# Four graph layers with pre-norm on one core: the normed inputs of layers 1 and 2 go through memory to be transposed

## The chip, the cores and the metric

The kernel runs on one core of one Trainium2 chip. The time is that of one execution on the device, in microseconds. The core has five engines that run side by side, each strictly in its own order: TensorE (PE, with its weight loads listed as PEld), VectorE (DVE), ScalarE (ACT), GpSimd (POOL) and SyncE (SP), which here does nothing but issue DMAs. They wait for each other by semaphores. [...]

## What is computed

There are 64 graphs of 256 nodes with 128 features, in fp32, and one adjacency matrix of 256 x 256 for all. Four layers follow each other; each adds its result to x, and each starts with the same norm:

```python
h = maximum(layernorm(x), 0); x = x + L0(h)   # and so on for L1, L2, L3
# L0: pre = s1[:, :, None] + s2[:, None, :] + b   (256 features, all pairs of nodes)
#     attn = softmax(sum_e a_e * leaky(pre_e) + adj);  sigmoid(attn @ h)
# L1: x_h = elu(h @ Wi + bi); e = sigmoid(a_tgt + a_src + be) * mask(adj)
#     recv = elu([e @ x_h, x_h * rowsum(e)] @ Wn + bn);  [recv, x_h] @ Wm + bm
# L2: A = exp(8 tanh(h q (h k)^T / sqrt(128) / 8)) * adj;  (A / rowsum(A)) @ h @ v
# L3: 5 steps of a gated unit: m = adj @ h; z, r = sigmoid(..); h = (1 - z) h + z tanh(..)
```

Layer 0 is by far the largest part: for every pair of nodes and each of 256 features a maximum has to be formed before the features are summed.

## The kernel before

**Groups and layers.** The 64 graphs are taken in 34 groups (`GROUPS`, line 15): 30 of two graphs, with two groups of one graph at each end. A group's x is a tile of 128 partitions x 4 blocks x 128 features; a block is half a graph's nodes. A `W` of 512 is the 4 blocks x 128 nodes of a group.

**Layer 0's pairs.** `Pairs` (from line 596) makes tiles `r` of 128 partitions x 256, each of them a maximum of `s2` and one column of `s1n`. Such a tile can be made by ACT (line 714), by POOL (719) or by DVE (696, eight or four at a time). A batch is eight tiles in one of `BUFS` = 12 buffers; PE multiplies a batch with `a_win` into `e_ps` (line 780). When `SPARE` = 5 batches are waiting for PE, the next two rows are merged: DVE adds the second feature's maximum onto the first (738), and PE has a batch less to do. `softmax0` then does the softmax, the product with h and the sum with x.

**Who sets the order.** The program is written out by a planner that runs when the kernel is built (the loop from line 1303). It has a clock for each of PE, DVE, ACT and POOL, charges each instruction a fixed cost, and always emits what can begin first. The work behind layer 0's pairs is written as generators ("chains") that yield the name of the engine they need next: `ahead` (norm and projections of the next group), `behind` (`softmax0`), `chain12` (layers 1 and 2), two `lanes` (layer 3 of even and odd groups) and two chains for the last two groups. A chain has a pace: its next step is due so many ns after the last one (2500 for `behind`, 2200 for `chain12`, 2100 for the lanes). A yield may name a condition and an earliest time. On the chip, each engine then keeps the emitted order, whatever is late.

**Transposes.** The products need h with features on the partitions, the norm leaves it with nodes there. The kernel has two ways:
- `transpose_blocks` (477): PE turns four blocks into PSUM (line 127), ACT copies them out (487). Layers 1 and 2 do so, each with its own norm `ln_relu` (442), as the first steps of `chain12`.
- `crossed` (89): SP issues a DMA that writes the tile to memory (`there`, line 93) and, when that has landed, a second DMA (95) that reads it back with the first two axes exchanged. For that the norm stores its output as features x blocks, `across=True`, so that the read moves 16 bytes (4 blocks) at a time. Layer 3 of groups 0 to 27 (`BY_MEMORY`, 26) does so, in `layer3_across` (1116): once behind its norm (`h3t`), and once at the end of each of four of the five steps (`hn`). After a crossing the planner lets the product that reads it begin no earlier than `TURN` = 28000 ns behind the producer. SP's DMAs are one queue in the order emitted: the loads of x, the crossings, the small `row` and `bound` transfers, and the writes of `out`.

**Tiles.** x lies in `xt` (line 140, five buffers). `softmax0` writes x1 over it; `layer1` makes `x1b` (x1 plus a bias, on POOL, line 900) and `x2`, `layer2` makes `x3`, layer 3 makes `y`, each a tile of its own. The adjacency is held twice: `adj_t` (columns half by half) for layers 1 and 2, and `adj_q` (node and half interleaved) for `layer3_across`. The helper `mm` (112) does each product as four products of 32 columns; in the trace an fp32 product shows as two records.

Of the kernel before, what the change touches and what calls it, by code (L numbers as in the profile page):

```python
# [24 lines left out]
TURN = 28000  # L25
BY_MEMORY = range(0, 28)
# [31 lines left out]
def kernel(ctx: ExitStack, tc: tile.TileContext, ins: dict, out: bass.AP):  # L58
# [127 lines left out]
    def numbers(shape, name, pattern, per_partition, t=None):  # L186
# [16 lines left out]
        for k, home in {  # L203
            "L2_gnn_q": ("hf_0", 2), "L2_gnn_k": ("hf_0", 2), "L3_gnn_w3_w": ("x1b",),
            "L3_gnn_w4_w": ("y1",), "L3_gnn_w5_w": ("x2",), "L3_gnn_u3_w": ("m_t",),
# [16 lines left out]
    adj_t = constant([P, 2, N], "adj_t")  # L222
    adj_q = constant([P, 2, P, 2], "adj_q")
    v2_rep = constant([P, P], "v2_rep")
# [6 lines left out]
    def constants0():  # L231
# [128 lines left out]
        t_ps = psum([P, 2, N], "adj_t_ps")  # L360
# [4 lines left out]
        dve(2 * N).tensor_copy(adj_t, t_ps)  # L365
# [13 lines left out]
    def constants1():  # L379

        for c in range(2):
            yield "dve"
            dve(N).tensor_copy(adj_q[:, :, :, c], adj_t[:, :, bass.ts(c, P)])
        yield "dve"

        dve(2 * N).tensor_scalar(mask_h, adj_t, 0.0, 0.5 * 0.005, ALU.is_equal, ALU.mult)
        yield "dve"
        dve(2 * N).scalar_tensor_tensor(mask_h, adj_t, 0.5, mask_h, ALU.mult, ALU.add)
# [24 lines left out]
        q_t, k_t = raw["L2_gnn_q"], raw["L2_gnn_k"]  # L413
        yield from transposed(q_t, q_t)
        yield from transposed(k_t, k_t)
        yield "pe"
        qk_ps = psum_a([P, P], "qk_ps")
        mm(qk_ps, lhsT=q_t, rhs=k_t, start=True, stop=True)
        yield "dve"
        dve(P).tensor_copy(qk, qk_ps)  # L420

        for k, t in ws.items():
            yield "dve"
            r = raw["L3_gnn_" + k]
            dve(P).tensor_tensor(r[:, 0:P], r[:, 0:P], r[:, P : 2 * P], ALU.add)
            yield from transposed(t, r[:, 0:P])
        yield from transposed(u3_t, raw["L3_gnn_u3_w"])
        yield from transposed(u5_th, raw["L3_gnn_u5_w"], 0.5)
        yield "dve"

        dve(P).tensor_tensor(w34_t, ws["w3_w"], ws["w4_w"], ALU.subtract)
        yield "dve"
        for t, a, b, scale in (
            (bz, "w3_b", "u3_b", 0.5), (br, "w4_b", "u3_b", 0.5), (bh, "w5_b", "u5_b", 1.0),
        ):
            dve(1).tensor_tensor(t, biases[a], biases[b], ALU.add)
            if scale != 1.0:
                dve(1).tensor_scalar(t, t, scale, None, ALU.mult)
# [346 lines left out]
    def softmax0(g, b, of, e_ps, snd):  # L785
# [43 lines left out]
        for ic in range(2):  # L829
# [5 lines left out]
        x1 = xt  # L835
        dve(N).scalar_tensor_tensor(
            x1[:, bass.ts(b, 2), :], o_ps, 0.5, xt[:, bass.ts(b, 2), :], ALU.mult, ALU.add
        )
        if b == GROUPS[g] - 1:
            chain12.add(first_rest(g, x1))  # L840
# [30 lines left out]
    def layer1(x1):  # L871
        G, NB, W = sizes(x1)
        h = yield from ln_relu(bp, x1, "h1", "h")
        h_t = yield from transpose_blocks(bp, h, "h_t", psum_a)
        yield "pe"
        xh_ps = psum_a([P, W], "xh_ps")
        mm(xh_ps, lhsT=wi, rhs=flat(h_t), start=True, stop=True)
        xh_t = yield from elu(xh_ps, bi, "xh_t", "xh_t")

        for b in range(NB):  # L880
# [17 lines left out]
        x1b = bp.tile([P, G, P], F32, tag="x1b", name="x1b")  # L898
        counts["x1"] += 1
        pool(1265).tensor_tensor(  # L900
            x1b, x1, bm_bc.unsqueeze(1).to_broadcast([P, G, P]), ALU.add
# [4 lines left out]
        for b in range(NB):  # L906
            yield "pe"
            th_ps = psum_a([P, 2, N], "th_ps")
            mm(th_ps[:, 0, :], lhsT=wt_rep, rhs=xh_t[:, bass.ts(b, N)], start=True, stop=True)
# [23 lines left out]
        for b in range(NB):  # L933
            for jc in range(2):
                mm(
                    rc_ps[:, bass.ts(b, N)], lhsT=y[:, b * 2 + jc, :], rhs=e_ts[b][:, jc, :],
                    start=(b == 0 and jc == 0), stop=False, skip_group_check=True,
                )
# [4 lines left out]
        for g in range(G):  # L943
            mm(
                o1_ps[:, g, :], lhsT=rc_t[:, bass.ts(g, P)], rhs=wm[:, 0, :], start=True, stop=False
            )
            mm(
                o1_ps[:, g, :], lhsT=xh_t[:, bass.ts(g, P)], rhs=wm[:, 1, :], start=False, stop=True
            )
        yield "dve"  # L950
        x2 = bp.tile([P, G, P], F32, tag="x2", name="x2")
        dve(W).tensor_tensor(x2, o1_ps, x1b, ALU.add)
        return x2

    def layer2(x2, when):
        G, NB, W = sizes(x2)
        h = yield from ln_relu(bp, x2, "h2", "h")
        h_t = yield from transpose_blocks(bp, h, "h_t", psum_a)
        yield "pe"
# [7 lines left out]
        for g in range(G):  # L967
            mm(hv_ps[:, g, :], lhsT=h_t[:, g, :], rhs=vw, start=True, stop=True)
# [5 lines left out]
        for b in range(NB):  # L974
            yield "pe"
            s_ps = psum_a([P, 2, N], "s2_ps")
            for mc in range(2):
                mm(
                    s_ps[:, mc, :], lhsT=h_t[:, b * 2 + mc, :], rhs=g_t[:, bass.ts(b, N)],
# [8 lines left out]
            dve(2 * N).tensor_tensor(pm, s_ps, adj_t, ALU.mult)  # L988
            pms.append(pm)
        for b in range(NB):  # L990
            yield "pe"
            o_ps = psum_a([P, 2, P + 1], "o2_ps")
            for c in range(2):
                for mc in range(2):
                    mm(
                        o_ps[:, c, :], lhsT=pms[b][:, mc, bass.ts(c, P)], rhs=hv[:, b * 2 + mc, :],
                        start=(mc == 0), stop=(mc == 1),
                    )
            yield "dve", when
            if b == 0 and when:  # L1000
                x3 = bp.tile([P, G, P], F32, tag="x3", name="x3", bufs=2)
            elif b == 0:
                x3 = rp.tile([P, G, P], F32, tag="r", name="x3")
            rv = sp.tile([P, 2], F32, tag="rv", name="rv")
            dve(2, more=120).reciprocal(rv, o_ps[:, :, P])
            for c in range(2):
                dve(P, 1).scalar_tensor_tensor(
                    x3[:, b * 2 + c, :], o_ps[:, c, 0:P], rv[:, c : c + 1],
                    x2[:, b * 2 + c, :], ALU.mult, ALU.add,
                )  # L1010
        return x3
# [26 lines left out]
    def layer3(x3, hn, h_t, home):  # L1038
        G, NB, W = sizes(x3)
        hf = flat(h_t)  # L1040
        for step in range(STEPS):
            yield "pe"
            m_ps = home.bank([P, W], "m_ps")
            for b in range(NB):
                for mc in range(2):
                    mm(
                        m_ps[:, bass.ts(b, N)], lhsT=hn[:, b * 2 + mc, :], rhs=adj_t[:, mc, :],
# [48 lines left out]
            if step < STEPS - 1:  # L1096
# [3 lines left out]
                for g in range(G):  # L1100
                    tr(tp[:, bass.ts(g, P)], hf[:, bass.ts(g, P)])
# [7 lines left out]
        for g in range(G):  # L1109
            tr(tp[:, bass.ts(g, P)], hf[:, bass.ts(g, P)])  # L1110
        yield "dve"
        y = home.tile(W, "hn", "y").rearrange("p (g n) -> p g n", g=G)
        dve(W).tensor_tensor(y, tp.rearrange("p (g n) -> p g n", g=G), x3, ALU.add)  # L1113
        return y

    def layer3_across(x3, lane):
# [64 lines left out]
        y = bp.tile([P, G, P], F32, tag="hn" + tag, name="y")  # L1181
        dve(W).tensor_tensor(y, tp, x3, ALU.add)
        inside.remove(lane)
        return y

    def first_rest(g, x1):
        x2 = yield from layer1(x1)

        x3 = yield from layer2(x2, None if g == len(GROUPS) - 1 else lambda: done3(g - 2))
        if g in BY_MEMORY:  # L1190
            lanes[g % 2].add(last_rest(g, x3))
            return
        tag = "_%d" % (g % 2)
        hn = yield from ln_relu(bp, x3, "h3", "hn" + tag, lambda: done3(g - 2))
        h_t = yield from transpose_blocks(bp, hn, "h3t", psum_a, tag="hf" + tag, bufs=2)
        lane = {len(GROUPS) - 1: chain5, len(GROUPS) - 2: chain4}.get(g, lanes[g % 2])
        lane.add(last_rest(g, x3, hn, h_t, Home(g)))
# [4 lines left out]
    def last_rest(g, x3, hn=None, h_t=None, home=None):  # L1202
        if home is None:
            y = yield from layer3_across(x3, g % 2)
        else:
# [5 lines left out]
            y = yield from layer3(x3, hn, h_t, home)  # L1211
            if not home.banks:
                inside.remove(g % 2)
        nc.sync.dma_start(out=of_group(out, g), in_=y)
        written.add(g)

    counts = {"w_p": 0, "left": 0, "x1": 0}
# [50 lines left out]
    lanes = [Chain(2100), Chain(2100)]  # L1268
# [34 lines left out]
    while True:  # L1303
        while to_load and counts["x1"] >= to_load[0] - 4:
# [111 lines left out]
```

## Time and profile before

| | us |
|---|---|
| median of 3 runs | 4993.88 (4990.81 to 4998.51) |
| the profiled execution, its own time | 4991.51 |
| its span (first to last instruction) | 4989.7 |
| PE busy | 4946.9 (99%) |
| DVE busy | 4865.1 (98%) |
| ACT busy | 4884.7 (98%) |
| POOL busy | 4771.1 (96%) |
| granted TensorE clock | 0.999 |

A line of the profile's groups has the source line, the engine, the operation, output<-inputs (buffer numbers left out), the shape and the count; behind the first bar the time in which the group was busy (us) and the mean duration of one (ns); behind the second the idle time of the engine just before them and what ended it. ACT and DVE overlap the end of one instruction with the beginning of the next, so the distance from start to start is shorter than the duration. In the timeline of SP the second column is how long the issue took; a DMA's data move after that.

The largest groups are the tiles of layer 0: 9944 on POOL (4520.5 us busy), 10232 on ACT (4541.5 us), 1351 instructions with 8 or 4 tiles each (2398.1 us) and 4168 merges (1729.2 us) on DVE, and 40816 records of their products on PE (3290.6 us). The DMA queue carries 140 crossings of 256 or 128 KB, each read in 16-byte or 8-byte packets: 2.29 of its 2.37 million packets.

### The profile page before, as it was taken

The numbers are of one execution on the slowest core, as the hardware profiler recorded it, in microseconds if no ns is written. First come the engines' busy times: TensorE is split into PE (matmuls) and PEld (weight loads), VectorE is DVE, ScalarE is ACT, GpSimd is POOL, SyncE is SP. The second block draws the span as 40 slices with busy tenths as digits, with TensorE's granted clock in tenths as the row PEclk, the third lists the DMA queues.
The fourth block names the chain that finished last, engine by engine and source line by source line (L and its number), as shares of the span: only waits on it lengthen the run. The fifth ranks groups of instructions, "written<-read, shape, count | busy, mean of one in ns | idle before, by whom it ended". The sixth has DMA issues, their size and how long they took to land. (4 is left out here: it accounts for less than half of the span.)

```text
span 4989.7 us, 176852 instructions
## 1 busy us (share of the span) xinstructions
PE 4946.9 (99%) x69759; PEld 2337.1 (47%) x69759; DVE 4865.1 (98%) x8327; ACT 4884.7 (98%) x12828; POOL 4771.1 (96%) x10569
## 2 busy tenths in 40 slices
PE   9999999999999999999999999999999999999997
PEld 4455444444544444444444444444454444444443
DVE  9999999999999999999999999999999999999994
ACT  8999999999999999999999999999999999999994
POOL 8999999999999999999999999999999999999882
PEclk9999999999999999999999999999999999999999
DMA  0144553654454555464444444353544434321000
GB/s 22 4 14 16 21 25 19 28 24 20 23 24 19 23 23 27 20 23 23 23 23 23 23 19 27 20 28 19 23 23 23 23 23 24 19 15 9 4 7 6
DMA packets 2372273, 100.40 MB, mean 20 GB/s; under 512 B 2318576, under 2 KB 2354800, under 8 KB 2371440
## 3 DMA queue, kind: packets, MB, share of 16 engines
q1 hardware_dynamic: 2370896, 88.83, 39.1%
q8 instruction: 547, 8.96, 0.9%
q14 instruction: 286, 2.34, 0.2%
q10 hardware_dynamic: 544, 0.26, 0.0%
HBM read 45.23 MB, written 43.84 MB: 18 GB/s over the span
## 5 line engine op out<-in xcount | busy, mean ns | idle before, releaser
L719 POOL TENSOR_SCALAR r<-s,s1n 128x256 f32<-128x256 f32 x9944 | 4520.5, 479 | 79.5 <-PE e_ps L780 36.1
L714 ACT ACTIVATE r<-s_act,s 128x256 f32<-128x256 f32 x9720 | 4226.5, 952 | 10.3 <-PE e_ps L780 10.0
L780 PE MATMUL e_ps<-r,a_win 128*32 128x256 f32 (+1 forms) x40816 | 3290.6, 465 | 5.5 <-DVE r L696 4.7
L696 DVE TENSOR_TENSOR r<-s_ps,s1n 128x2048 f32<-128x2048 f32 (+1 forms) x1351 | 2398.1, 1821 | 2.8 <-PE e_ps L780 2.6
L780 PEld LDWEIGHTS e_ps<-r,a_win 128*32 128x32 f32 x40816 | 1339.9, 110 | 1590.3 <-issue 846.0
L738 DVE SCALAR_TENSOR_TENSOR r<-s_ps,s1n,r 128x256 f32<-128x256 f32 x4168 | 1729.2, 485 | 2.9 <-POOL r L719 2.7
L714 ACT ACTIVATE r<-s,s 128x256 f32<-128x256 f32 x512 | 315.0, 1145 | 0.0
L120 PE MATMUL m_ps<-adj_q,hn 128*32 128x256 f32 x3456 | 209.2, 380 | 0.0
L120 PE MATMUL gate_ps<-m_t,t_w_w 128*32 128x512 f32 (+1 forms) x1360 | 170.6, 571 | 4.0 <-ACT m_t L1054 2.9
L120 PEld LDWEIGHTS m_ps<-adj_q,hn 128*32 128x32 f32 x3456 | 135.2, 135 | 79.2 <-issue 30.2
L471 ACT ACTIVATE h<-x,bsh,brs 128x128 f32<-128x128 f32 x256 | 159.0, 865 | 13.0 <-POOL bsh L464 9.0
L120 PE MATMUL hv_ps<-rh,u_th 128*32 128x512 f32 (+1 forms) x1360 | 169.6, 567 | 1.5 <-DVE rh L1067 1.5
L120 PE MATMUL gate_ps<-m_t,w_t 128*32 128x512 f32 (+1 forms) x1360 | 169.9, 568 | 0.7 <-ACT m_ps L1064 0.6
L120 PE MATMUL hv_ps<-m_t,t_w_w 128*32 128x512 f32 (+1 forms) x1360 | 170.1, 569 | 0.0
L471 ACT ACTIVATE h<-xt,bsh,brs 128x128 f32<-128x128 f32 x256 | 158.5, 916 | 3.8 <-POOL bsh L464 2.5
L1143 ACT COPY m_t<-m_ps 128x512 f32<-128x512 f32 (+1 forms) x140 | 159.9, 1142 | 0.0
L1159 ACT ACTIVATE gate_ps<-gate_ps,bz 128x512 f32<-128x512 f32 (+1 forms) x140 | 159.6, 1140 | 0.0
L1161 ACT ACTIVATE hv_ps<-hv_ps,bh 128x512 f32<-128x512 f32 (+1 forms) x140 | 153.4, 1096 | 0.0
L1147 ACT ACTIVATE m_ps<-gate_ps,br 128x512 f32<-128x512 f32 (+1 forms) x140 | 152.7, 1091 | 0.0
L120 PE MATMUL gate_ps<-hf,u_t 128*32 128x512 f32 (+1 forms) x1088 | 138.0, 575 | 0.0
L120 PE MATMUL s_ps<-h0t,w_p 128*32 128x256 f32 (+1 forms) x1568 | 134.7, 444 | 0.8 <-ACT h0t L487 0.5
L462 POOL TENSOR_TENSOR brs<-bve,neg_half 128x4 f32<-128x4 f32 (+1 forms) x136 | 133.7, 983 | 0.0
(231 smaller groups left out, 4527.8 us busy)
## 6 DMA issues: line engine op xcount, KB each, us to landing
there<-hf SPq DMA_DIRECT2D x104, 256.0 KB
hn<-there SPq DMA_DIRECT2D x104, 256.0 KB
xt<-in_x_dram SPq DMA_DIRECT2D x30, 256.0 KB
out_dram<-y SPq DMA_DIRECT2D x30, 256.0 KB
there<-h SPq DMA_DIRECT2D x26, 256.0 KB
h3t<-there SPq DMA_DIRECT2D x26, 256.0 KB
row<-rows SPq DMA_DIRECT2D x128, 0.5 KB
there<-hf SPq DMA_DIRECT2D x8, 128.0 KB
```

What stands on the lines that cost most here:

```text
L120: nc.tensor.matmul(out[bass.ts(c, 32)], lhsT=lhsT[:, bass.ts(c, 32)], rhs=rhs, **flags)
L462: pool(1085).tensor_tensor(rstd, ve, neg_half[:, 0:G], ALU.pow)
L471: act(P, 2, 1).activation(h[:, :, g] if across else h[:, g, :], xt[:, g, :], AF.Relu, bias=shift[:, g : g + 1], scale=rstd[:, g : g + 1],)
L696: nc.vector.tensor_tensor(r[:, 2 * g2 : 2 * g2 + n, :, :], s2[:, ec : ec + 1, :].unsqueeze(1).to_broadcast([P, n, 2, N]), s1n.to_broadcast ...
L714: nc.scalar.activation(r[:, g, ic, :], s2[:, ec, :], AF.Relu, bias=s1[:, ec, i : i + 1])
L719: nc.gpsimd.tensor_scalar(r[:, g, ic, :], s2[:, ec, :], FLT_MAX, s1n[:, ec, i : i + 1], ALU.min, ALU.max,)
L738: nc.vector.scalar_tensor_tensor(r[:, g, ic, :], self.own("dve")[:, 1, :], self.of["s1n"][:, 1, i : i + 1], r[:, g, ic, :], ALU.max, ALU.add,)
L780: nc.tensor.matmul(to, lhsT=a_win[:, sign, 31 - t : 63 - t], rhs=of, start=False, stop=self.over, skip_group_check=True,)
L1143: act(W).copy(m_t, m_ps)
L1147: act(W, 1).activation(m_ps, g_ps, AF.Tanh, bias=br, scale=0.5)
L1159: act(W, 1).activation(g_ps, g_ps, AF.Tanh, bias=bz, scale=0.5)
L1161: act(W, 1).activation(hv_ps, hv_ps, AF.Tanh, bias=bh)
```

## The change

Layers 1 and 2 of groups 0 to 31 get their transposed input by `crossed`; only the last two groups still use PE (`by_pe`). Layer 1's norm is now run at the end of `softmax0`'s chain (`first_norm`), which issues the crossing and then hands the rest to `chain12` with the earliest time of the first product. `TURN` goes from 28000 to 16000, for all crossings, layer 3's included. Layer 3 crosses in groups 0 to 28 instead of 0 to 27; the lanes' pace is 2300 instead of 2100.

As a crossing of 16-byte runs leaves node and block interleaved, all tiles of layers 1 and 2 are in that order now (`pairs`): weights such as `xh[:, :, g]` are read with a step, some products write PSUM with a step, and the masks come from `adj_q`; `adj_t` is gone. x1 plus bias, x2, x3 and y are written over x in `xt`, which has eight buffers instead of five; the load of a group's x waits until the group eight before it has been written out.

```diff
-TURN = 28000
-BY_MEMORY = range(0, 28)
+TURN = 16000
+BY_MEMORY = range(0, 32)
+BY_MEMORY_3 = range(0, 29)
...
-        xt = ap.tile([P, 2 * GROUPS[g], P], F32, tag="xt", name="xt", bufs=5)
+        xt = ap.tile([P, 2 * GROUPS[g], P], F32, tag="xt", name="xt", bufs=8)
...
         if b == GROUPS[g] - 1:
-            chain12.add(first_rest(g, x1))
+            yield from first_norm(g, xt)
...
-    def layer1(x1):
+    def layer1(x1, h, h_t, at):
         G, NB, W = sizes(x1)
-        h = yield from ln_relu(bp, x1, "h1", "h")
-        h_t = yield from transpose_blocks(bp, h, "h_t", psum_a)
-        yield "pe"
+        if h_t is None:
+            h_t = yield from by_pe(h, "h_t1")
+        yield "pe", None, at
         xh_ps = psum_a([P, W], "xh_ps")
         mm(xh_ps, lhsT=wi, rhs=flat(h_t), start=True, stop=True)
...
-                    y_ps[:, c, :], lhsT=xh_t[:, bass.ts(2 * b + c, P)], rhs=wn1,
+                    y_ps[:, c, :], lhsT=xh[:, :, 2 * b + c], rhs=wn1,
...
-                    rsum_ps[:, bass.ts(b, N)], lhsT=ones, rhs=e_ts[b][:, jc, :],
+                    pairs(rsum_ps)[:, :, bass.ts(b, 2)], lhsT=ones, rhs=pairs(e_ts[b][:, jc, :]),
...
-                o1_ps[:, g, :], lhsT=rc_t[:, bass.ts(g, P)], rhs=wm[:, 0, :], start=True, stop=False
+                o1_ps[:, g, :], lhsT=pairs(rc_t)[:, :, g], rhs=wm[:, 0, :], start=True, stop=False
...
-    def layer2(x2, when):
+    def layer2(x2, by_memory):
         G, NB, W = sizes(x2)
-        h = yield from ln_relu(bp, x2, "h2", "h")
-        h_t = yield from transpose_blocks(bp, h, "h_t", psum_a)
-        yield "pe"
+        h = yield from ln_relu(bp, x2, "h2", "h", across=True)
+        at = model.t["act"] + TURN
+        h_t = crossed(h, "h_t", "h_t") if by_memory else (yield from by_pe(h, "h_t"))
+        yield "pe", None, at if by_memory else None
...
+    def first_norm(g, xt):
+        h = yield from ln_relu(bp, xt, "h1", "ln", across=True)
+        h_t = at = None
         if g in BY_MEMORY:
-            lanes[g % 2].add(last_rest(g, x3))
+            h_t = crossed(h, "h_t1", "h_t")
+            at = model.t["act"] + TURN
+        chain12.add(first_rest(g, xt, h, h_t, at))
...
-    lanes = [Chain(2100), Chain(2100)]
+    lanes = [Chain(2300), Chain(2300)]
...
-        while to_load and counts["x1"] >= to_load[0] - 4:
+        while to_load and done3(to_load[0] - 8):
             xts.append(load_x(to_load.pop(0)))
```

More of the change, by code (lines that the diff above doesn't have):

```diff
@@ L869, in elu_1, with by_pe, pairs @@
         return o
-    def layer1(x1):
+    def by_pe(h, tag, bufs=None):
+        yield "pe"
+        G = h.shape[2]
+        tp = psum_a([P, P, G], "h_t_ps")
+        turn()
+        for g in range(G):
+            tr(tp[:, :, g], h[:, :, g])
+        yield "act"
+        t = bp.tile([P, P, G], F32, tag=tag, name="h_t", bufs=bufs)
+        act(P * G).copy(t, tp)
+        return t
+    def pairs(t):
+        return t.rearrange("p (q g) -> p q g", q=P)
+    def layer1(x1, h, h_t, at):
         G, NB, W = sizes(x1)
-        h = yield from ln_relu(bp, x1, "h1", "h")
-        h_t = yield from transpose_blocks(bp, h, "h_t", psum_a)
-        yield "pe"
+        if h_t is None:
+            h_t = yield from by_pe(h, "h_t1")
+        yield "pe", None, at
         xh_ps = psum_a([P, W], "xh_ps")
@@ L878, in layer1 @@
         xh_t = yield from elu(xh_ps, bi, "xh_t", "xh_t")
+        xh = pairs(xh_t)
         for b in range(NB):
@@ L897, in layer1 @@
         yield "pool"
-        x1b = bp.tile([P, G, P], F32, tag="x1b", name="x1b")
-        counts["x1"] += 1
         pool(1265).tensor_tensor(
-            x1b, x1, bm_bc.unsqueeze(1).to_broadcast([P, G, P]), ALU.add
+            x1, x1, bm_bc.unsqueeze(1).to_broadcast([P, G, P]), ALU.add
         )
@@ L908, in layer1 @@
             th_ps = psum_a([P, 2, N], "th_ps")
-            mm(th_ps[:, 0, :], lhsT=wt_rep, rhs=xh_t[:, bass.ts(b, N)], start=True, stop=True)
+            mm(
+                pairs(th_ps[:, 0, :]), lhsT=wt_rep, rhs=xh[:, :, bass.ts(b, 2)],
+                start=True, stop=True,
+            )
             for jc in (1, 0):
@@ L967, in layer2 @@
         for g in range(G):
-            mm(hv_ps[:, g, :], lhsT=h_t[:, g, :], rhs=vw, start=True, stop=True)
+            mm(hv_ps[:, g, :], lhsT=h_t[:, :, g], rhs=vw, start=True, stop=True)
         yield "act"
@@ L978, in layer2 @@
                 mm(
-                    s_ps[:, mc, :], lhsT=h_t[:, b * 2 + mc, :], rhs=g_t[:, bass.ts(b, N)],
+                    pairs(s_ps[:, mc, :]), lhsT=h_t[:, :, b * 2 + mc],
+                    rhs=pairs(g_t)[:, :, bass.ts(b, 2)],
                     start=True, stop=True,
@@ L995, in layer2 @@
                     mm(
-                        o_ps[:, c, :], lhsT=pms[b][:, mc, bass.ts(c, P)], rhs=hv[:, b * 2 + mc, :],
+                        o_ps[:, c, :], lhsT=pairs(pms[b][:, mc, :])[:, :, c], rhs=hv[:, b * 2 + mc, :],
                         start=(mc == 0), stop=(mc == 1),
                     )
[L999 to L1003, printed above, removed]
+            yield "dve"
             rv = sp.tile([P, 2], F32, tag="rv", name="rv")
@@ L1046, in layer3 @@
                     mm(
-                        m_ps[:, bass.ts(b, N)], lhsT=hn[:, b * 2 + mc, :], rhs=adj_t[:, mc, :],
+                        pairs(m_ps)[:, :, bass.ts(b, 2)], lhsT=node(hn, b * 2 + mc),
+                        rhs=adj_q[:, mc, :, :],
                         start=(mc == 0), stop=(mc == 1),
```

84 lines of the change are left out of this document (42 added, 42 removed).

## The prediction

> **What bounds the kernel now.** I read the busy shares first, then the stretches, then the groups, then the DMA queue's timeline. The page begins with (shares of the span; then tenths in 40 slices):
>
> ```profile
> PE 4946.9 (99%) x69759; PEld 2337.1 (47%) x69759; DVE 4865.1 (98%) x8327; ACT 4884.7 (98%) x12828; POOL 4771.1 (96%) x10569
> ...
> DMA  0144553654454555464444444353544434321000
> ...
> q1 hardware_dynamic: 2370896, 88.83, 39.1%
> ```
>
> No engine has room. In the stretch from 2000 to 3000 us PE is busy 999.2 of 1000, DVE 992.8, ACT 998.6, POOL 983.4. PE's busy time is modelled, so I checked it: a round of four 32-column products of 256 columns starts 0.216 us after the last one, one of 512 columns 0.429 us; all products and transposes of the program at such rates fill 99.3% of PE's time in mid-run, so it has 0.7% to spare. The planner keeps the four level, because the relu tiles `r` can be made by ACT, POOL or DVE, and merging spares PE at DVE's cost. So neither one engine's saving nor one engine's wait stays on that engine. Only the DMA engines have room (39.1%). PE works strictly in the planner's order, and the planner only assumes a delay (`TURN`) for a crossing through memory; if the data are later than assumed, PE stands still and nothing else can be slipped in.
>
> How long a crossing takes is in the DMA queue's timeline (start, length, issue). A lone one, then two that meet:
>
> ```profile
> 2042.07 0.33 SPq L93 DMA_DIRECT2D there<-hf  x1
> 2044.15 0.36 SPq L95 DMA_DIRECT2D hn<-there  x1
> ```
> ```profile
> 2279.78 0.35 SPq L93 DMA_DIRECT2D there<-h  x1
> 2282.23 0.36 SPq L95 DMA_DIRECT2D h3t<-there  x1
> 2282.69 9.99 SPq L93 DMA_DIRECT2D there<-hf  x1
> 2294.41 0.36 SPq L95 DMA_DIRECT2D hn<-there  x1
> ```
>
> Alone: `hf` is done at 2042.04, the write is issued 0.03 us later, the read 2.1 us after that, and the 16-byte packets stop at 2055.1. With the 0.43 us that pass between a write's last packet and the read's issue, the data can be used 13.5 us after the producer. Over all isolated crossings the read takes 10.9 us (9.6 to 11.7). Meeting: SP has to wait for the first write before it issues the first read, and the second write's issue then hangs for 9.99 us behind the first read's packets. The second read is issued 12.2 us after the first and its packets stop at 2305.4, 23.8 us after its producer (2282.04). So a second crossing whose producer comes d later is ready after about 25.5 - d us. Today that costs nothing: the trace shows 27.8 us or more between every producer and the first product that reads its crossing (median 29.4 for `hn`, with TURN 28), and the waits list has 0.6 us of PE waiting for a crossing in the whole run.
>
> **Part 1, work removed and re-dealt.** From the order of both programs; times are start-to-start medians in the trace's timeline.
> - ACT: 61 fewer copies of 512 columns out of the transposes (57 `h_t`, 4 `h3t`), 4 fewer `hn`, 4 fewer of 256: 65 x 0.466 + 4 x 0.26 = -31.3; 4 more tiles at 0.357: +1.4. Sum -30 us.
> - POOL: 56 fewer tiles at 0.454: -25 us. The in-place bias add costs what `x1b` cost (1.29 us).
> - DVE: 216 fewer merges at 0.392 (-84.7), 29 more whole and 9 more half batches at 2.197 and 1.131 (+73.9): -11 us.
> - PE: 268 fewer transposes at 0.152 (-40.7); less merging adds 216 products of 256 columns, two records each, 0.055 us (+23.8): -17 us.
> The three makers lose 22 us on the mean. The tail gives a little back: behind the last tile ACT has 7 us more to do, PE 8. I take **-20**. The rewritten `adj_q`, the masks and the in-place x are the same sizes as before: nothing. Layer 1's norm keeps its instructions; moved, it is six more steps of the softmax chain (pace 2.5 us, 15 us a group), which at 11 steps a graph fills 55 us of the 153 a group takes: it fits, and what stands behind it, the next graph's softmax, is due a whole graph later. Without that room the cost would be 15 us a group.
>
> **Part 2, strided operands.** `h_t`, `xh_t`, `rc_t` become weights read with 16 bytes between elements, `pm` with 8.
>
> ```profile
> L120 PEld LDWEIGHTS m_ps<-adj_q,hn 128*32 128x32 f32 x3456 | 135.2, 135 | 79.2 <-issue 30.2 <-PE e_ps L780 2.8 <-DVE r L738 2.7
> L120 PEld LDWEIGHTS o_ps<-wm,rc_t 128*32 128x32 f32 x1024 | 31.1, 110 | 15.9 <-issue 10.8 <-DVE r L738 1.8 <-DVE rc_t L868 1.5
> ```
>
> A strided load takes 135 ns instead of 110. Under a 256-column round (216 ns, the same for `m_ps` with and without the stride) it is hidden. But 768 products have only 128 or 129 columns (y1 128, o1 256, hv 128, o2 256), 2 rounds each, and their rounds start every 109 ns: no row shows a strided load there. Bounds: 0 if something hides it, 26 ns x 1536 = 40 us if the load sets the pace. The nearest row is the strided transpose of `y_ps`, 120 ns from one to the next where contiguous ones take 109: 11 x 1536 = 17 us. I take 17, all on PE, which just uses up PE's -17; as the saving of the makers can then not be had in full, +8 in the sum. A gain below zero is excluded, since no load becomes shorter. Strided writes to PSUM (`rsum_ps`, `rc_ps`, `s_ps`) cost nothing by the `m_ps` row, whose output has the same step.
>
> [...]
>
> **Part 3, the new waits.** The element-wise crossings rise from 140 to 209, so the DMA share goes to 39.1 x 209/140 = 58%. SP issues 138 DMAs more in the one queue; the loads of x (now into eight buffers) and the `bound` rows behind them are planned two groups and 30 us ahead, which covers a crossing of 12 us. That alone would fit, and engines do not slow down beside the transfers: POOL's tiles start 455 ns apart on the mean in microseconds full of packets and 460 in others. But TURN falls to 16. In the new order ACT has 18.5 us of work (median of 32, 17.6 to 20.8) between layer 2's last `h` and the copy of `g_ps`; its chain's step of 2.2 us lies after the product, so the product stands at 16.3. A lone crossing (13.5) makes that.
>
> The pairs do not. The norm of layer 1, now in the softmax chain, and the norm of layer 3 come out of ACT almost together: in 28 of 29 groups their crossings follow each other directly in SP's order, with producers 0.8 to 6.7 us of ACT work apart (mean 3.1). Half the time layer 1 is second, half layer 3. Where layer 1 is second, `xh_ps` stands at 16.4 + 0.7 and the data come at 25.5 - 2.9: 5.5 us late, 14 times. Where layer 3 is second, `gate_ps` stands behind 1.7 us of `m_ps`, at 18.1, the data come at 25.5 - 3.3: 4.1 us late, 14 times. Together 135 us. PE today runs some 1.1 us behind plan (29.4 against 28.3), which takes 28 x 1.1 off: 104. Layer 2's crossing also meets `hn` crossings: 0 to 30, I count 10. Queued behind the waiting product are the tile products; buffers free for the makers last about 3 us, and ACT's next operation on a PE result comes within some 6 us with a slack of 0.7 (median): so ACT and DVE stop too, and the shift stays. With 0.7% to spare PE wins back about 0.5 us between two pairs, 14 in all. **+100** us; 0 at least (no wait makes anything faster), 165 at most.
>
> **Sum:** 4991.5 (the profiled execution: span 4989.7 plus 1.8; the median of three is 4993.9) - 20 + 8 + 100 = 5079.5. For the median, 2.4 above, I forecast **5080**.
>
> **Rivals.**
> - *Slower, by colliding crossings* (the forecast): 0.77. From 4993.9: 5012 if PE can fall 4 us behind the other engines without stopping them (28 x 0.8 + 8 of stalls, -20, +8), 5132 with all 135 us of the pairs and 40 us of weights on PE (net 23), -20.
> - *Faster: the waits are absorbed.* Each engine's order has enough work between, and the data miss PE by less than what buffers cover: -20 + (0 to 8) gives 4974 to 4982. For it: lone crossings are in time, and the planner keeps up to five ready batches, 0.87 us of PE work each, so the makers go on for a while. Against: PE's order is fixed, and ACT and DVE wait for PE soon after. It decides if pairs come less than 3 us late. 0.16.
> - *Same:* the strided weights (17 to 40) eat the saved work, with no stalls: 4984 to 5004. 0.07.
> - That the transposes do not go away is excluded by the order (256 `h_t_ps` transposes become 24).
>
> **Numbers.** What a measurement of this kernel can tell from no change is about 0.2%, 10 us. Range 4978 to 5130: it leaves out some 12% below (the better part of the absorbed case) and 5% above.
>
> **What would show it.** Right: PE waits for `h_t` and `h3t` crossings, 4 to 5 us each, some 28 of them, 90 to 140 us together; a write on SP that hangs about 8 us in every pair; PE busy 97% in mid-run; h_t copies gone from ACT; loads of `xh_t`, `rc_t` at 135 ns and rounds of 120. Wrong: PE's wait for crossings under 30 us, or `xh_ps` more than 22 us after its `h`; then the work of part 1 decides and the time is below 4985.

## The result and the profile after

The changed kernel takes 5347.98 us (median of 4 runs, 5339.71 to 5350.61), the kernel before 4996.19 in the same measurement (4990.81 to 5000.52): 1.0705 times as long, 95% interval 1.0692 to 1.0719. The forecast was 5080, its range ended at 5130. The direction was right, and so was the mechanism of the waits; the size was not: 352 us instead of 86. The waits were longer and more than counted, and a cost that follows 45 of them, some us with the granted TensorE clock at 0.50, was in no term.

Two lines of the page of after, the busy shares and the DMA queue:

```profile
PE 5031.7 (94%) x69923; PEld 2356.4 (44%) x69923; DVE 4862.3 (91%) x8147; ACT 4879.6 (91%) x12763; POOL 4747.4 (89%) x10513
...
q1 hardware_dynamic: 3512432, 123.97, 53.8%
```

DVE, ACT and POOL are busy for as many us as before (within 24); their shares fall together because the span grew from 4989.7 to 5345.3. In the stretch from 2000 to 3000 us (busy us of PE, PEld, DVE, ACT, POOL; then granted clock, DMA share, GB/s) no engine is full any more:

```profile
2000.00:3000.00 1000.00, 941.55 (x13052) 439.21 (x13045) 919.24 (x1544) 923.21 (x2413) 903.24 (x1997) 0.97 0.63 28
```

The list of PE's waits (total us, times, longest) names what PE stands still for. The page's chain of work that ended last has transfers in it, which had no share of it before:

```profile
PE g_ps L121 <- DMA h_t<-there: 103.8, 26, 7.8
PE xh_ps L121 <- DMA h_t<-there: 90.8, 14, 9.2
PE gate_ps L121 <- DMA h3t<-there: 70.4, 13, 10.0
```
```profile
PE 57%; DMA 20%; ACT 10%; DVE 10%; POOL 2%; issue 2%; SPq 0%; ACTq 0%; DVEq 0%; POOLq 0%
```

`xh_ps` is layer 1's first product, `g_ps` layer 2's, `gate_ps` layer 3's. One pair, first in SP's timeline (start, length of the issue), then PE's at the same place:

```profile
2652.96 0.33 SPq L94 DMA_DIRECT2D there<-h  x1
2654.98 0.36 SPq L96 DMA_DIRECT2D h3t<-there  x1
2655.39 8.74 SPq L94 DMA_DIRECT2D there<-h  x1
2667.63 0.36 SPq L96 DMA_DIRECT2D h_t<-there  x1
```
```profile
2669.39 1.91 PE L121 MATMUL m_ps<-adj_q,h 128*32 128x256 f32 x32
2671.12 1.04 PE L121 MATMUL gate_ps<-h3t,u_t 128*32 128x512 f32 x8
2679.23 1.93 PE L121 MATMUL xh_ps<-h_t,L_gnn_Wi 128*32 128x512 f32 x8 [7.07 <-DMA h_t<-there]
2680.94 1.93 PE L779 MATMUL e_ps<-r,a_win 128*32 128x512 f32 x8
```

Layer 3's `h` crosses first. Layer 1's write is issued 0.4 us behind its read, hangs 8.7 us, its read starts at 2667.6, and the data land 11 us later. PE reached `xh_ps` at 2672.2 and stood for 7.07 us. Then look at the lengths: eight records of 512 columns take 1.04 us as `gate_ps`, ahead of the wait, and 1.93 us as `xh_ps`, behind it. The granted clock (the share of its full rate that TensorE was given) in three stretches, the wait, the 4 us behind it and the next 4 us (columns as above):

```profile
2672.00:2679.00 7.00, 0.16 (x4) 0.00 (x0) 1.93 (x1) 3.65 (x10) 6.41 (x15) 0.71 1.40 58
2679.00:2683.00 4.00, 3.77 (x20) 0.99 (x24) 1.76 (x4) 0.98 (x2) 0.00 (x0) 0.50 0.67 21
2683.00:2687.00 4.00, 4.00 (x44) 1.43 (x40) 3.53 (x9) 2.52 (x7) 2.07 (x5) 0.74 1.62 31
```

The clock falls to 0.50 in the course of the wait and stays there for some us after it (4.4 on the mean of the waits that show it). The trace's records of the granted clock show 50 such spells, 320.7 us in all, 45 of them ahead of the last tile of layer 0; before there were 16.7 us, all behind the last tile. 106.9 us of the 320.7 lie in PE's idle time and cost nothing; in the other 213.8 PE works at half speed and loses 106.9 us of work (8.1 before).

So the 355.6 us of span are: PE idle 310.2 in place of 39.5 (+270.7; counted up to PE's last product) and PE busy +84.8, which is the half clock (+98.8) less 14 us of work that is gone.

### The profile page after: what moved, and what is told of

Its sections match the earlier page's. It is cut to its first block, busy times and chain, and to the rows that moved or that the text cites. A ratio compares the mean times of both kernels' runs of the same rounds, so it can differ in the third digit from the quotient of the medians.

```text
span 5345.3 us, 177152 instructions
## 1 busy us (share of the span) xinstructions
PE 5031.7 (94%) x69923; PEld 2356.4 (44%) x69923; DVE 4862.3 (91%) x8147; ACT 4879.6 (91%) x12763; POOL 4747.4 (89%) x10513
## 4 chain that ended last, share of the span: by engine, by line
PE 57%; DMA 20%; ACT 10%; DVE 10%; POOL 2%; issue 2%; SPq 0%; ACTq 0%; DVEq 0%; POOLq 0%
PE e_ps L779 31%; DMA h_t<-there 9%; DMA there<-h 9%; ACT r L713 7%; PE gate_ps L121 6%; PE hv_ps L121 5%; DVE r L695 4%; DVE r L737 3%; PE m_ps L121 3%; DMA h3t<-there 3%; PE s_ps L121 3%; PE e_ps L121 2%; ACT h L470 2%; POOL r L718 1%; PE o_ps L121 1%
## 5 line engine op out<-in xcount | busy, mean ns | idle before, releaser
L713 ACT ACTIVATE r<-s_act,s 128x256 f32<-128x256 f32 x9724 | 3939.2, 754 | 22.6 <-PE e_ps L779 21.3
L779 PE MATMUL e_ps<-r,a_win 128*32 128x256 f32 (+1 forms) x41248 | 3355.9, 470 | 6.5 <-DVE r L695 5.7
L695 DVE TENSOR_TENSOR r<-s_ps,s1n 128x2048 f32<-128x2048 f32 (+1 forms) x1389 | 2459.9, 1812 | 11.4 <-PE e_ps L779 8.3
L779 PEld LDWEIGHTS e_ps<-r,a_win 128*32 128x32 f32 x41248 | 1375.7, 111 | 1693.4 <-issue 936.5
L737 DVE SCALAR_TENSOR_TENSOR r<-s_ps,s1n,r 128x256 f32<-128x256 f32 x3952 | 1631.5, 472 | 1.6 <-POOL r L718 1.4
L470 ACT ACTIVATE h<-xt,bsh,brs 128x128 f32<-128x128 f32 x512 | 295.7, 829 | 20.6 <-POOL bsh L463 15.3
L713 ACT ACTIVATE r<-s,s 128x256 f32<-128x256 f32 x512 | 259.7, 708 | 0.0
L121 PE MATMUL m_ps<-adj_q,hn 128*32 128x256 f32 x4096 | 251.4, 384 | 2.6 <-ACT hn L1123 2.3
L121 PE MATMUL g_ps<-h_t,qk 128*32 128x512 f32 (+1 forms) x272 | 46.5, 755 | 103.8 <-DMA h_t<-there 103.8
L121 PE MATMUL xh_ps<-h_t,L_gnn_Wi 128*32 128x512 f32 (+1 forms) x272 | 47.7, 752 | 90.9 <-DMA h_t<-there 90.8
```

Of the source, the lines that this page charges most:

```text
L121: nc.tensor.matmul(out[bass.ts(c, 32)], lhsT=lhsT[:, bass.ts(c, 32)], rhs=rhs, **flags)
L470: act(P, 2, 1).activation(h[:, :, g] if across else h[:, g, :], xt[:, g, :], AF.Relu, bias=shift[:, g : g + 1], scale=rstd[:, g : g + 1],)
L695: nc.vector.tensor_tensor(r[:, 2 * g2 : 2 * g2 + n, :, :], s2[:, ec : ec + 1, :].unsqueeze(1).to_broadcast([P, n, 2, N]), s1n.to_broadcast ...
L713: nc.scalar.activation(r[:, g, ic, :], s2[:, ec, :], AF.Relu, bias=s1[:, ec, i : i + 1])
L737: nc.vector.scalar_tensor_tensor(r[:, g, ic, :], self.own("dve")[:, 1, :], self.of["s1n"][:, 1, i : i + 1], r[:, g, ic, :], ALU.max, ALU.add,)
L779: nc.tensor.matmul(to, lhsT=a_win[:, sign, 31 - t : 63 - t], rhs=of, start=False, stop=self.over, skip_group_check=True,)
```

## The experiments

**Theory.** PE's products are placed before the data of meeting crossings can be there (271 us of waits), and 45 of the 51 waits of over 0.7 us are followed by a stretch at half clock (99 us). **Rivals:** 1, the transfers themselves slow the engines; 2, strided or in-place tiles cost the time; 3, TURN 16 is too short even for a lone crossing; 4, the half clock has no price of its own; 5, it is the number of crossings, not where they meet; 6, the moved norm of layer 1 makes the pairs. All ratios are to the kernel before, run beside; its median was between 4987.9 and 4997.4 us, so gains between runs of different sittings are better read from the ratios than from the times.

**Layers 1 and 2 turned by PE, TURN 28000.**

```diff
-TURN = 16000
-BY_MEMORY = range(0, 32)
+TURN = 28000
+BY_MEMORY = range(0)
```

> The changed kernel with layers 1 and 2 turned by PE in every group (BY_MEMORY empty, so by_pe is used throughout) and TURN 28000: what is left of the change is the interleaved tiles, x1, x2, x3 and y written over x, layer 1's norm in the softmax chain and layer 3's crossing in one group more. The planner's clock ends 1 us later than that of the kernel before. Theory (late crossings): 4985 to 5010, as the kernel before. Rival 2 (strided or in-place tiles cost the time): well above 5100. My own term for the strided weights in the prediction, 17 us on PE, would show as 5010 to 5020; if it is 0, as 4990 to 5000.

Measured: 4991.56 us, ratio 0.9998 (0.9989 to 1.0007); PE idle 33 us. Strided weights and PSUM writes, interleaved order and x written over itself cost, with what else is left of the change, nothing that this run can tell from zero (its interval is some 5 us each way). Rival 2 falls.

**The kernel before with TURN 16000.**

```diff
-TURN = 28000
+TURN = 16000
```

> The kernel before with TURN 16000 instead of 28000: only layer 3's 140 crossings, with the short delay. The planner's clock ends 10 us earlier. Theory (a lone crossing is usable 13.5 us behind its producer, and only meeting ones are late): two lanes meet only by chance; 70% or more of the 140 are lone and in time, PE waits 0 to 60 us in all, time 4985 to 5060, PE's mean wait per crossing under 0.5 us. Rival 3 (16 us is too short even for a lone crossing, whatever it meets): nearly every crossing waits, 140 waits of 2 us or more, time above 5200.

Measured: 4980.00 us, ratio 0.9975 (0.9966 to 0.9984), faster than I expected: PE waits for a crossing once, for 0.4 us. Lone crossings are in time, so rival 3 falls, and the shorter delay alone is worth 12 us, which no term of my sum had.

**Idle products in the waits.** The order is that of the changed kernel; only PE's wait is filled.

```diff
...
+    def fill(p, name):
+
+        for k in range(LATE[name].get(met[name], 0)):
+            for c in range(4):
+                nc.tensor.matmul(
+                    p[bass.ts(c, 32)], lhsT=wi[:, bass.ts(c, 32)],
+                    rhs=flat(mask_h)[:, 0 : p.shape[1]], start=True, stop=True,
+                )
...
+        fill(xh_ps, "xh_ps")
...
```

`LATE` holds how many go in front of which product; `g_ps` and `gate_ps` have the same call.

> The changed kernel in exactly its order, with 127 idle products of 512 columns (1.72 us each, 215 us in all) put in front of the 46 products that waited longest in its trace, each place getting as many whole ones as its wait there had room for. They write the PSUM tile that the waiting product then overwrites, and the planner is not charged. Theory with the clock as a cause of its own: data come as late as before, but PE is not idle, so the granted clock stays up: PE idle 310 -> 80 to 130 us, half clock 321 -> under 80 us, and the time falls by 60 to 100 us, to 5250 to 5290, though PE has 215 us more to do. Rival 4 (the half clock costs nothing of its own, the waits alone set the time; or the clock falls for another reason, such as the transfers): the time stays within 15 us of 5348, or rises.

Measured: 5303.27 us, ratio 1.0625 (1.0608 to 1.0643): 45 us less than the changed kernel (40 by the ratios), but above what I expected. My size of the filling was wrong: four products of 512 columns in two records each take 0.86 us together, not 1.72, so only 109 of the 265 us were filled (PE idle 310 to 193). Half clock fell to 160 us, the lost work from 107 to 70, by 37. That goes with the theory, but half a dose doesn't decide it.

> The same as the fill before it with 277 idle products in place of 127: in the run just seen a product of 512 columns took 0.86 us and not 1.72, so that only half of each wait was filled (109 us of products, PE idle 193, half clock 160, time 5303). Now some 238 us in the same 46 places. Theory (the half clock that follows a wait has its own price): PE idle 60 to 100 us, half clock under 70 us in place of 321 in the changed kernel, lost work under 40 us in place of 107, time 5245 to 5285. Rival 4 (the clock has no price of its own): not under 5300.

Measured: 5262.02 us, ratio 1.0548 (1.0533 to 1.0564). PE is now nearly as full as before the change, and the granted clock is 0.996:

```profile
PE 5173.9 (98%) x72139; PEld 2465.9 (47%) x72139; DVE 4859.8 (92%) x8147; ACT 4877.3 (93%) x12763; POOL 4747.5 (90%) x10513
...
PE g_ps L138 <- DMA h_t<-there: 31.5, 18, 4.5
PE xh_ps L138 <- DMA h_t<-there: 8.4, 9, 2.0
PE gate_ps L138 <- DMA h3t<-there: 6.3, 4, 2.0
```

Half clock 41 us in place of 321, lost work 19 in place of 107: 88 us less, and the time is 86 us less (78 by the ratios), though PE has some 240 us more to do. The order and the transfers are the same. Rival 4 falls: some 80 to 90 us of the loss are the clock's, the rest the waits'. This is no way to gain time, only to tell the two apart.

**A planner that keeps account of SP's queue.** The same crossings and operands; the product's earliest time comes from the queue instead of a constant.

```diff
-TURN = 16000
+TURN = 15000
+WRITE, READ, AFTER = 2100, 11300, 1500
...
+    queue = {"sp": 0.0, "moved": 0.0}
+
+    def behind_reads(now):
+
+        queue["sp"] = max(now, queue["sp"])
+        queue["sp"] = max(queue["sp"], queue["moved"] - 800)
+
+    def lands(now):
+
+        behind_reads(now)
+        queue["sp"] += WRITE
+        queue["moved"] = queue["sp"] + READ
+        return max(now + TURN, queue["moved"] + AFTER)
...
-            at = model.t["act"] + TURN
+            at = lands(model.t["act"])
...
+        behind_reads(model.t["dve"])
         nc.sync.dma_start(out=of_group(out, g), in_=xt)
```

> The changed kernel with a planner that keeps account of SP's queue: the write of a crossing or of an output is held until 0.8 us before the read ahead of it has moved its data, a crossing's read is issued 2.1 us behind its write and needs 11.3 us, and the product may begin 1.5 us after that, 15 us behind the producer at the least. Nothing else changes, and the planner's clock ends 20 us earlier than that of the kernel before. Theory (what costs the time is products placed before the data of meeting crossings can be there): with the same 209 crossings and the same operands PE's waits for crossings fall from 271 us to 0 to 40, PE idle to 40 to 80 us, half clock under 60 us, and the time to 4960 to 5000. Rival 1 (the traffic) and rival 2 (strided or in-place tiles): above 5200.

Measured: 4963.08 us, ratio 0.9951 (0.9935 to 0.9968), faster than both kernels. From its page and PE's waits:

```profile
PE 4917.7 (99%) x69747; PEld 2478.4 (50%) x69747; DVE 4848.5 (98%) x8215; ACT 4860.0 (98%) x12791; POOL 4730.8 (95%) x10533
...
q1 hardware_dynamic: 3512432, 123.97, 57.9%
...
PE m_ps L136 <- DMA hn<-there: 3.3, 5, 1.0
```

The transfers are the same, packet for packet, in a shorter span (57.9% of it), and crossings still meet: 63 writes of crossings hang for over 1 us on SP, 70 in the changed kernel. A pair of it, SP and then PE:

```profile
2594.85 0.50 SPq L109 DMA_DIRECT2D there<-h  x1
2598.64 0.36 SPq L111 DMA_DIRECT2D h3t<-there  x1
2599.06 10.15 SPq L109 DMA_DIRECT2D there<-h  x1
2610.90 0.36 SPq L111 DMA_DIRECT2D h_t<-there  x1
```
```profile
2624.07 0.60 PE L136 MATMUL xh_ps<-h_t,L_gnn_Wi 128*32 128x512 f32 x3
```

The second read is issued 16.1 us behind the first write (14.7 in the pair above), and `xh_ps` stands 13.2 us behind it, when the data are there. PE had other work up to then. Rival 1 falls: the meetings and the traffic cost nothing that shows where the product is placed by them. So does rival 5, as all 209 crossings are there.

**TURN 20000 and 24000 in the changed kernel** (one constant each).

> The changed kernel with TURN 20000. The planner's clock ends 6 us earlier than that of the kernel before. Theory: each of the 46 long waits, 5.7 us on the mean, becomes some 4 us shorter if the same crossings meet; what is left is some 60 to 130 us, and few of the waits are long enough for the clock to fall, so half clock 20 to 120 us; time 5040 to 5150. Rival 1 or 2: within 30 us of 5348.

Measured: 5059.13 us, ratio 1.0143 (1.0128 to 1.0158); PE idle 112 us, half clock 61. The time was as expected, the place wasn't: 61.6 us of waits stand at `m_ps`, for `hn` crossings, which had not waited at 16000, and 6.3 at `g_ps`. A new delay makes a new order, and other crossings meet.

> The changed kernel with TURN 24000. The planner's clock ends 2 us later than that of the kernel before. Theory: a second crossing is there 25.5 us less the distance of the producers behind its producer, the product stands some 1 us behind TURN, so at most a few waits of 1 to 3 us are left where a third transfer is in the way: 0 to 50 us in all, hardly any half clock beyond the end of the kernel, time 4990 to 5045. Rival 1 or 2: above 5200.

Measured: 4990.60 us, ratio 1.0004 (0.9995 to 1.0013); one wait of 2.2 us for a crossing, PE idle 52 us. That it isn't below the kernel before lies at the end: the last tile of layer 0 is done at 4827 us in place of 4887, but 144 us instead of 90 pass from its last product to the end of the span.

With TURN 28000, the delay of the kernel before, there is no time for the changed kernel: the order that the planner then makes ends in a deadlock, and which engines block each other I didn't trace. So the delay is tried at 20000 and 24000 only.

**One layer at a time, TURN 16000.**

```diff
-        h_t = crossed(h, "h_t", "h_t") if by_memory else (yield from by_pe(h, "h_t"))
-        yield "pe", None, at if by_memory else None
+        h_t = crossed(h, "h_t", "h_t") if False else (yield from by_pe(h, "h_t"))
+        yield "pe"
```

> The changed kernel (TURN 16000) with layer 2 turned by PE again; layers 1 and 3 still cross. The planner's clock ends 22 us earlier than that of the kernel before. Theory: the 28 pairs of layer 1 and layer 3 are made by their two norms and stay; in the changed kernel they waited 169 us, and layer 2's 102 us go with its crossing. So PE waits 120 to 200 us, half clock 120 to 230 us, time 5110 to 5240. Rival 5 (no pair is at fault, it is the sum of 209 crossings in one queue that overloads it): with 178 crossings PE waits under 50 us and the time is under 5030.

Measured: 5109.43 us, ratio 1.0230 (1.0215 to 1.0245), just under the expected range. Rival 5 falls here too, as fewer crossings wait all the same, and so does a part of my theory: the pairs don't stay as they were.

```profile
PE xh_ps L121 <- DMA h_t<-there: 121.1, 13, 17.1
```

Layer 3's `gate_ps` doesn't wait at all, its `m_ps` 1.7 us. Layer 1 has few waits, but long ones: in seven of them it is third, behind `h3t` and `hn`, each further crossing ahead of it adding some 12 us to SP's queue (in one of them the three reads are issued at 2638.2, 2650.2 and 2662.0 us). The clock cost less for each us of these waits: of 130 us of half clock 78 lie within PE's idle time, so 26 us of work are lost beside 123 us of waits, where the changed kernel lost 97 beside 271.

```diff
-        if g in BY_MEMORY:
+        if False:
             h_t = crossed(h, "h_t1", "h_t")
```

> The changed kernel (TURN 16000) with layer 1 turned by PE again, its norm still in the softmax chain; layers 2 and 3 still cross. The planner's clock ends 6 us later than that of the kernel before. Theory: layer 2's crossings keep meeting the `hn` crossings of the lanes, as they did in the changed kernel (102 us in 23 waits), the pairs are gone: PE waits 60 to 130 us, half clock 60 to 150 us, time 5070 to 5180. My prediction counted 10 us for these meetings: by it the time would be 4990 to 5030. Rival 5 (overload by number): under 5030 as well.

Measured: 5119.58 us, ratio 1.0245 (1.0230 to 1.0260).

```profile
PE g_ps L121 <- DMA h_t<-there: 88.2, 25, 7.7
```

Layer 2's product waits nearly as long as in the changed kernel (103.8 us). It needs no pair of norms: the lanes' `hn` crossings are enough.

**The queue's account with smaller margins, and with the lanes' old pace.**

> The planner that keeps account of the queue, with 0.5 us in place of 1.5 between the landing it works out and the product, and 14.5 us in place of 15 as the least delay. The planner's clock ends 2 us later than with 1.5 us. Theory: a lone crossing is usable 13.5 us behind its producer, so both margins still cover it; a few waits under 1.5 us may come, too short for the clock to fall; 4960 to 4985. If the account of the queue is off by over 1 us in the meetings, 20 to 60 waits of about 1 us: 4985 to 5030.

Measured: 4983.71 us, ratio 0.9974 (0.9963 to 0.9985); 12 us of waits for crossings, the longest 2.3.

> The planner that keeps account of the queue, with 1.5 us as before and the lanes' pace at 2100 as in the kernel before. The planner's clock ends 3 us later than with 2300. Theory: no waits for crossings either way, so the pace is worth what the planner's clock says: 4960 to 4980. If the slower pace of the lanes was what kept crossings apart: waits of 50 us or more, above 5010.

Measured: 4979.42 us, ratio 0.9969 (0.9957 to 0.9981); 4 us of waits for crossings. Both times are as expected, and both are slower than the first version, by 9 to 12 us by the ratios, whose intervals overlap with its own. Their last tiles are 12 to 15 us later. I have no run that tells why; that the first version is the best of the three is not shown beyond doubt.

**Layer 1's norm and crossing back in the chain of layers 1 and 2.**

```diff
-            yield from first_norm(g, xt)
+            chain12.add(first_norm(g, xt))
...
-        chain12.add(first_rest(g, xt, h, h_t, at))
+        yield from first_rest(g, xt, h, h_t, at)
```

> The changed kernel (TURN 16000, all three layers crossing) with layer 1's norm and its crossing put back into the chain of layers 1 and 2, where each begins when the group before has left the chain, just as layer 3's norm of that group begins. The planner's clock ends 27 us later than that of the kernel before and 43 us later than that of the changed one, because the chain now also holds the 16 us of layer 1's delay. Theory: the pairs do not come from the softmax chain; the two norms start together here too, so crossings still meet, PE waits 120 to 300 us and the time is 5150 to 5400. Rival 6 (moving layer 1's norm to the softmax chain is what made the pairs): the waits on `xh_ps` and `gate_ps` go from 169 us to under 30, those on `g_ps` stay near 100, time 5120 to 5170.

Measured: 5421.62 us, ratio 1.0858 (1.0840 to 1.0876), some 20 us above what I expected, with 303 us of waits for crossings:

```profile
PE gate_ps L121 <- DMA h3t<-there: 108.4, 17, 8.7
PE g_ps L121 <- DMA h_t<-there: 104.5, 27, 7.2
PE xh_ps L121 <- DMA h_t<-there: 89.8, 13, 8.5
```

Rival 6 falls: where layer 1's norm is run doesn't make the meetings.

## Why the prediction was right and wrong

- **What bounds the kernel: right.** With all engines full, PE's stalls came out as time. POOL, the engine with the most tiles to wait for, shows 258 us of waiting for PE to free tile buffers.
- **Part 1, -20: the sign is likely, the size isn't shown.** Without waits the change is worth 25 us (4963.08 against 4987.85), but 12 us came with the shorter delay alone in the kernel before, and the end of the kernel moves by tens of us with the order. PE's own work fell by 14 us, where I had 17.
- **Part 2, strided weights, 17 on PE (+8 in the sum): nothing for the weights.** The loads take 135 ns, as predicted:

```profile
L121 PEld LDWEIGHTS o_ps<-wm,rc_t 128*32 128x32 f32 x1024 | 35.1, 135 | 14.9 <-issue 8.8 <-DVE r L737 2.4 <-DVE rc_t L866 1.1
```

  But the rounds of 128 columns that they feed didn't get longer: the 1024 records of these products fill 28.0 us from start to start in both kernels. The nearest row (the transposes' 120 ns) misled; the lower bound was the value. The PSUM writes of `rsum_ps` and `rc_ps`, two elements out of every four, cost nothing either, as the row of `m_ps` had said: 216 ns a round in both kernels. `s_ps` was put beside them by mistake. Its output lies in one piece; what is strided is the operand that streams through, `pairs(g_t)[:, :, bass.ts(b, 2)]`, in runs of 8 bytes 16 bytes apart. Its rounds take 230 ns in place of 216 (medians, start to start), those of `th_ps`, with `xh` read the same way, 229; the kernel with layers 1 and 2 turned by PE reads `g_t` and `xh` in the same runs. In the groups, before and after (a few records of after stand at half clock, so its mean is a little high):

```profile
L120 PE MATMUL s_ps<-g_t,h_t 128*32 128x256 f32 x1024 | 67.2, 380 | 0.1
L121 PE MATMUL s_ps<-g_t,h_t 128*32 128x256 f32 x1024 | 71.5, 394 | 0.5 <-ACT hv L989 0.5
```

  These are 384 rounds, some 5 us of PE in all, too few for the second experiment to show.
- **Part 3, the pairs, 104: mechanism and count right, size too small.** `xh_ps` waits 14 times and `gate_ps` 14 times, exactly the 28 events counted from the order (the list above has 13 for `gate_ps`, as it puts one of 7.5 us down to a DVE tile that had long been made). In all of them the second crossing stands directly behind the first on SP, and it is the second that is late. They last 90.8 and 77.9 us, 169 together: 6.5 and 5.6 us each, where I had 5.5 and 4.1 and then took off 1.1. Two steps failed. One is "PE today runs some 1.1 us behind plan": PE reached `xh_ps` 17.2 us behind its `h` and `gate_ps` 17.9 us (means), where the plan had 17.1 and 18.1, so there was no lag to take off (31 us). The other is the data's time: they came 23.7 and 23.5 us behind their `h`, where 25.5 - d with the mean distances gave 22.6 and 22.2 (33 us).
- **Part 3, layer 2, "0 to 30, I count 10": 102.** This is the largest mis-sized wait. I looked for pairs among norms and let layer 2's crossing meet `hn` by chance. In the 23 waits of over 0.7 us its write stands behind another crossing's write by 2 to 13 us, in 15 of them with the write of `out` between:

```profile
1586.40 0.33 SPq L94 DMA_DIRECT2D there<-hf  x1
1588.47 0.36 SPq L96 DMA_DIRECT2D hn<-there  x1
1588.88 10.57 SPq L1239 DMA_DIRECT2D out_dram<-xt  x1
1599.55 0.45 SPq L94 DMA_DIRECT2D there<-h  x1
1602.09 0.36 SPq L96 DMA_DIRECT2D h_t<-there  x1
```

  In this view of SP in the changed kernel layer 2's `h` was done at 1590.5, 4.1 us behind the write of `hf`; the write of `out` hangs behind the `hn` read, and layer 2's own write is issued only 9 us behind its producer; `g_ps` waits 7.07 us. I had counted SP's DMAs, but not followed who is next to whom in its order for this crossing, as I had for the pairs. With layer 2 crossing beside layer 3 alone the same waits are there (88 us).
- **Part 3, what follows a wait: a step missing altogether, 99.** A wait was priced at its own length. The two fillings show the other price: 78 to 86 us went when PE was kept busy in the same waits. The trace of before could not show it, as its clock never fell ahead of the end. The trace of after does: ahead of the last tile every wait for a crossing above 3.7 us was followed by a spell at half clock, and seven from 2.7 to 3.7 us were. The price was 97 us of lost work for the 45 spells, 2.2 us each.
- **Catching up, -14: hardly seen.** PE's idle time besides the waits for crossings was 39.5 us before and is 37.5 after, so 2 us were won back. The whole loss is then 169 (pairs) + 102 (layer 2) + 99 (clock) - 14 (work): 4991.5 + 356 = 5347.5, and the profiled execution took 5347.07. That the two agree is no proof of the parts, as PE's idle and busy time make up the span in any case.
- **Engines don't slow beside transfers: right**, by the planner with the queue's account, which carries them all in 4963 us.

So the range failed at its upper end: it let all waits together reach 165 (135 for the pairs and 30 for layer 2), where 271 came, and had no room for a second price on each. The rival *faster* would have needed data less than 3 us late, *same* no stalls.

What stays open: which crossings meet is decided by the whole order, and I can't derive it from a single edit. TURN 20000, one layer alone, or the norm in another chain each gave other waits in other places. Hardly any were left with the planner's account of the queue, which places each product by what is ahead of it, or with a delay of 24000 for every crossing. How its 25 us divide into shorter delay, saved work and the shape of the end I didn't separate.

## What to carry to other kernels

Where one queue carries transfers of some 11 us one behind the other, as here, a delay measured on a lone transfer is not a delay for the next one: follow the queue's order for every consumer, add up what is ahead of it, and place the consumer by that sum. Where TensorE is full, price a long wait at more than its length, here by 2.2 us on the mean behind 45 of the 46 waits for a crossing of 2.7 us and more. And before a loss is put down to traffic or strides, look whether the same traffic and strides cost anything in an order that doesn't wait.

## What the runs showed of the hardware

- The granted clock falls to 0.5 some 3.6 us (2.1 to 5.1) behind the beginning of a wait and comes back 4.4 us (2.6 to 6.0) behind its end (45 waits of the changed kernel). 49 of its 50 spells last 3.41, 6.83 or 10.24 us, one, two or three times one length: of the 45, the 12 behind waits of 2.7 to 4.2 us last 3.41 (nine) or 6.83, the 33 behind waits of 4.5 to 10.0 us 6.83 or 10.24 (seven). From 20 us of the span on (the clock's record begins at 12.5), every wait above 3.7 us was followed by a spell; of the 11 gaps between 0.7 and 3.7 us that were not, ten were under 2.0.
- A write issued behind an element-wise read hung on SP until 0.7 us (median) before that read's last packet was through: up to 10.5 us, 70 times over 1 us in the changed kernel. A write of `out` did the same (23 times, up to 10.6 us), and what came next on SP was issued behind it. A read of 256 KB in 16-byte packets took 10.9 us (median; 9.6 to 11.9) in the changed kernel, meetings and all, as long as the isolated ones of the kernel before (10.9): meeting crossings queued and didn't slow each other.
- Weights read with 16 bytes between elements took 135 ns to load in place of 110, and rounds of four products as short as 109 ns were not held up by it. An operand that streams through in runs of 8 bytes 16 bytes apart made a round of 256 columns 230 ns in place of 216 (`s_ps`; `th_ps` 229); a PSUM output written in such runs left it at 216 (`rsum_ps`, `rc_ps`).
